# Transposing softmax exponentials in four 32-row strips of TensorE instead of two 64-row strips, under a newly written order

## The chip, the cores and the metric

The kernel runs on one core of a Trainium2 chip. The metric is the device time of one execution in microseconds (us), as the median of several runs. All durations below come from one profiled execution of the kernel before the change. Engine names are those of the profile: PE is TensorE's matmul stream and PEld its stream of weight loads, DVE is VectorE, ACT ScalarE, POOL GpSimd, SP SyncE (which issues the DMAs).

## The reference

Eight sequences of 512 tokens (width 256) go through four residual blocks, each on a layer-normed input: a cross attention over a context of 1024 tokens (16 heads of 64), a feed-forward network that picks 2 of 8 experts per sequence, a second cross attention over the same context (16 heads of 16), and a feed-forward network with weights rounded to 8 bits and activations to 16. Only the first attention is touched:

```python
scores = jnp.einsum('bhqd,bhkd->bhqk', q, k) * SCALE
attn = jax.nn.softmax(scores, axis=-1)
out = jnp.einsum('bhqk,bhkd->bhqd', attn, v)
out = out.transpose(0, 2, 1, 3).reshape(B, NQ, INNER)
return out @ w_out + b_out
```

Everything is float32.

## The kernel before

**First attention.** `first_attention` (line 591) loops over n, 8 sequences by 8 pairs of heads, and within it over i, the four tiles of 128 queries. One tile (n, i) passes through five steps:

- `scores` (L721): for both heads, scores of 128 queries (rows) by 1024 keys (columns) in two PSUM tiles (L728). Each head uses 64 rows of the array, so the two heads run side by side. VectorE takes the row minimum of the negated scores (L739), ScalarE the exponential with its row sum (L741).
- `divide` (L752), one tile later: VectorE inverts the sums (L755), GpSimd multiplies each exponential by its share, 1024 columns per head (L758).
- `turn` (L667), two tiles later: the queries stand on the partitions, but the product with the values needs keys there. TensorE transposes the tile against an identity. The exponentials are the stationary operand (the weight load), the identity the moving one. A call handles half of the keys (u = 0 or 1): 2 heads by 4 key tiles by 2 halves of the queries (w), each a transpose of 64 partitions by 128 columns into a `[128, 64]` piece (L676). The halves w lie on different rows of the array and write different PSUM banks. One PSUM tile of two banks holds the result of a call. ScalarE (u = 0, L690) or VectorE (u = 1, L688) copies it to an `et` tile in SBUF.
- `attend` (L692): for two query tiles together, values times transposed exponentials, accumulated over 8 key tiles (L699). The heads use all 128 rows and 64 columns each.
- `project` (L710) adds the output product to the residual (L486).

In between lie `queries` (pq, L602), `keys` (pk, L512 and L514) and `values` (pv, L512 and L514) for later pairs. The last two run a first chunk on 128 rows and a second one on 64.

**Second stream.** The second attention of one sequence (L937) runs beside the first attention of the next. Its steps are `scores` (L562 and L565, tile s_c) together with `maxima` (L524, tile sm_c, with a VectorE maximum, L531), both on 64 rows by 128 columns for each of two parts, `attend` (cav, L1079, 128 rows by 32 columns for each of four parts), and small transposes and projections (tm_c, cf, cta, cacc).

**What sets the order.** TensorE's program is written out by hand. Each stream is a Python generator that yields before every step, and `weave` (L53) takes steps from the two streams in turn: `ORDER` (L27) lists how many steps of the first, then of the second, then of the first. TensorE executes the steps in just this order. The lists yielded with each step hold prices for a planner that made ORDER offline: microseconds on TensorE, engine and time of the eviction, and a word for the shape of the array ("full", "rows" for 64-row parts, "columns", "slots"). In the program they have no effect: `weave` counts steps and looks only at callables. The other engines run their instructions in the order in which the steps issue them.

**Buffers.** All PSUM tiles rotate through four buffers of two banks (`ps_s`, L129). A tile waits until the tile four allocations earlier has been read. The `et` tiles share two buffers of 8 KB per partition (tag "t"), and for the last sequence the second attention's split keys (L1032) reuse them.

Of the kernel before, what the change touches and what calls it, by code (L numbers as in the profile page):

```python
# [8 lines left out]
F32 = mybir.dt.float32  # L9
I32 = mybir.dt.int32  # L10
U32 = mybir.dt.uint32
F32R = mybir.dt.float32r
# [6 lines left out]
P = 128  # L19
# [5 lines left out]


ORDER = """  # L27
15 4 11 1 1 4 3 2 2 1 5 4 3 1 8 1 6 1 3 1 3 1 3 1 1 1 1 1 6 1 3 1 1 1 1 1 1 1 3 1 1
1 1 1 3 1 1 1 5 1 1 1 3 1 1 1 1 1 3 1 1 1 1 1 1 1 3 1 1 1 1 1 1 1 4 1 91 1 4 4 6 1 3
2 6 2 4 2 7 5 4 2 1 1 4 1 1 1 1 5 1 1 5 2 3 7 1 3 6 2 3 7 1 1 1 2 6 2 3 10 1 4 1 1 5  # L30
2 3 7 1 1 1 2 5 2 1 1 1 1 3 2 2 3 5 2 1 1 3 1 1 2 4 9 2 1 3 2 11 2 4 1 7 2 2 1 3 6 3
1 1 1 5 1 1 2 4 2 5 4 6 1 4 1 2 1 3 1 1 1 5 2 3 4 6 1 3 2 6 2 4 2 7 5 4 2 1 1 4 1 1
1 1 5 1 1 5 2 3 7 1 3 6 2 3 7 1 1 1 2 6 2 3 10 1 4 1 1 5 2 3 7 1 1 1 2 5 2 1 1 1 1 3
2 2 3 5 2 1 1 3 1 1 2 4 9 2 1 3 2 11 2 4 1 7 2 2 1 3 6 3 1 1 1 5 1 1 2 4 2 5 4 6 1 4
1 2 1 3 1 1 1 5 2 3 4 6 1 3 2 6 2 4 2 7 5 4 2 1 1 4 1 1 1 1 5 1 1 5 2 3 7 1 3 6 2 3
7 1 1 1 2 6 2 3 10 1 4 1 1 5 2 3 7 1 1 1 2 5 2 1 1 1 1 3 2 2 3 5 2 1 1 3 1 1 2 4 9 2
1 3 2 11 2 4 1 7 2 2 1 3 6 3 1 1 1 5 1 1 2 4 2 5 4 6 1 4 1 2 1 3 1 1 1 5 2 3 4 6 1 3
2 6 2 4 2 7 5 4 2 1 1 4 1 1 1 1 5 1 1 5 2 3 7 1 3 6 2 3 7 1 1 1 2 6 2 3 10 1 4 1 1 5
2 3 7 1 1 1 2 5 2 1 1 1 1 3 2 2 3 5 2 1 1 3 1 1 2 4 9 2 1 3 2 11 2 4 1 7 2 2 1 3 6 3
1 1 1 5 1 1 2 4 2 5 4 6 1 4 1 2 1 3 1 1 1 5 2 3 4 6 1 3 2 6 2 4 2 7 5 4 2 1 1 4 1 1  # L40
1 1 5 1 1 5 2 3 7 1 3 6 2 3 7 1 1 1 2 6 2 3 10 1 4 1 1 5 2 3 7 1 1 1 2 5 2 1 1 1 1 3
2 2 3 5 2 1 1 3 1 1 2 4 9 2 1 3 2 11 2 4 1 7 2 2 1 3 6 3 1 1 1 5 1 1 2 4 2 5 4 6 1 4
1 2 1 3 1 1 1 5 2 3 4 6 1 3 2 6 2 4 2 7 5 4 2 1 1 4 1 1 1 1 5 1 1 5 2 3 7 1 3 6 2 3
7 1 1 1 2 6 2 3 10 1 4 1 1 5 2 3 7 1 1 1 2 5 2 1 1 1 1 3 2 2 3 5 2 1 1 3 1 1 2 4 9 2
1 3 2 11 2 4 1 7 2 2 1 3 6 3 1 1 1 5 1 1 2 4 2 5 4 6 1 4 1 2 1 3 1 1 1 5 2 3 4 6 1 3
2 6 2 4 2 7 5 4 2 1 1 4 1 1 1 6 1 1 2 4 1 1 1 3 1 2 1 3 2 1 1 2 3 3 2 5 1 1 2 6 2 3
2 1 1 6 4 5 1 1 2 6 2 3 2 1 1 7 1 4 4 5 2 4 1 7 1 5 2 3 1 2 2 3 7 1 3 4 2 3 7 2 2 1
1 1 1 1 11 2 1 1 1 1 5 1 8 1 2 3 3 1 2 1 7 3 2 4 3 8 3 1 5 2 1 7 2 3 7 2 3 7 2 3 7 3
3 9 3 2 9 3 2 6 2 1 2 1 2 1 3 1 4 2
"""  # L50


# [26 lines left out]
def kernel(  # L79
# [26 lines left out]
    nc = tc.nc  # L106
    B, S, D = x.shape
    L, DC = cross.shape[1:]
    NT = S // P
    NK = L // P  # L110
# [18 lines left out]
    ps_s = ctx.enter_context(tc.tile_pool(name="ps_s", bufs=4, space=PSUM))  # L129
# [5 lines left out]
    ident = const.tile([P, P], F32, name="ident")  # L135
# [364 lines left out]
    def tok(t):  # L500
        return slice(t * P, (t + 1) * P)
# [89 lines left out]
    def first_attention():  # L591
# [72 lines left out]
            if half and m < last // 2:  # L664
                load_weights(m + 1, "v")

        def turn(n, i, u):  # L667


            j = i // 2  # L670
            t = ps_s.tile([P, 2, 2, 4, 64], F32, tag="s", name=f"t_{n}_{i}_{u}")
            for h in range(2):
                for kt in range(4):
                    for w in range(2):
                        half = slice(w * 64, (w + 1) * 64)
                        nc.tensor.transpose(  # L676
                            t[:, w, h, kt, :],
                            es[n, i][h][half, tok(4 * u + kt)],
                            ident[half, half],
                        )  # L680
            if i % 2 == 0:
                turned[n, j, u] = pp.tile(
                    [P, 2, 4, 2, 2, 64], F32, tag="t", name=f"et_{n}_{j}_{u}", bufs=2
                )
            dst = turned[n, j, u][:, :, :, i % 2].rearrange("p h k w s -> p w (h k) s")
            src = t.rearrange("p w h k s -> p w (h k) s")
            if u:
                nc.vector.tensor_copy(dst, src)  # L688
            else:
                nc.scalar.copy(dst, src)  # L690

        def attend(n, j):  # L692

            m, at = divmod(n * 2, G)
            av = bank(f"av_{n}_{j}")
            for u in range(2):
                for kt in range(4):
                    for h in range(2):
                        nc.tensor.matmul(  # L699
                            av[h * AD : (h + 1) * AD, : S // 2],  # L700
                            v[m][:, 4 * u + kt, (at + h) * AD : (at + h + 1) * AD],
                            turned[n, j, u][:, h, kt].rearrange("p i w s -> p (i w s)"),
                            start=(u == 0 and kt == 0),
                            stop=(u == 1 and kt == 3),
                        )
            if j == 0:
                o[n] = op.tile([P, S], F32, tag="o", name=f"o_{n}", bufs=3)
            nc.scalar.copy(o[n][:, j * (S // 2) : (j + 1) * (S // 2)], av[:, : S // 2])
# [55 lines left out]
        VALUES = [(2.75, "s", "act", 1.03, "full")]  # L764
        OUT = [(3.44, "s", "dve", 1.25, "full")]
        BIAS = [(0, None, "pool", 2.9, "aside")]
        TURN = 0.55

        share = 1 / (NP * NT)

# [8 lines left out]
        def divided(g):  # L779
            return [  # L780
                (0, None, "dve", 0.2, None, (("y", g % 4),), None),
                (0, None, "pool", 4.8, "then", (), ("w", g % 4)),
            ]

        def turned_round(g, u):
            engine, took = ("dve", 1.22) if u else ("act", 1.03)
            return [(TURN, "s", engine, took, "rows", (("w", g % 4),), ("t", u, g % 4))]

        def attended(g):

# [8 lines left out]
        for n in range(last + 2):  # L799
            b, p = divmod(n, NP)  # L800
            if n == 2:
                yield lambda: "biases" in done
                yield 0, BIAS
                bias()
            for i in range(NT):
                g = n * NT + i
                if n <= last:
                    yield 0, scored(g), share
                    scores(n, i)
                if n == 0 and i < 2:  # L810
                    yield 0, VALUES
                    values(0, i)


                if g > 3 and i % 2 == 0:
                    m = (g - 4) // NT
                    yield 0, attended(g - 3)
                    attend(m, i // 2)
                if i == 1 and p == NP - 2 and b + 1 < B:
                    yield from all_of(front[1 + DH :])  # L820
                if i == 1 and n // 2 + 1 <= last // 2:
                    yield 0, VALUES
                    values(n // 2 + 1, p % 2)
                if i == 3 and n < last:
                    yield 0, KEYS
                    keys(n + 1)
                if i == 3 and n % 2 == 0 and n > 0:
                    yield 0, OUT
                    project(n // 2 - 1)
                    if p == 0 and b < B:  # L830
                        done.add(b - 1)
                if 1 < g <= last * NT + NT + 1:
                    for u in range(2):
                        yield 0, turned_round(g - 2, u)
                        turn((g - 2) // NT, (g - 2) % NT, u)
                if 0 < g <= last * NT + NT:
                    yield 0, divided(g - 1)
                    divide((g - 1) // NT, (g - 1) % NT)
                if n > last:
                    if i == 3:  # L840
                        return
                    continue
                if i == 2 and n < last:
                    yield 0, QUERIES
                    queries(n + 1)

                if b + 1 < B:
                    if p == NP - 2:
                        if i == 0:
                            yield lambda: b == 0 or (b - 1, "stacked") in done  # L850
                            front, bias = prologue(b + 1)
                        elif i == 2:
                            yield from all_of(front[:1])
                    if p == NP - 1 and i == 0:
                        yield from all_of(front[1 : 1 + DH])
                        yield 0, BIAS
                        bias()
# [79 lines left out]
    def second_attention(b, pairs, last=False):  # L937
# [78 lines left out]
        def keys_of(m):  # L1016
# [12 lines left out]
                ]  # L1029
            )  # L1030
            if b == B - 1:
                both = pp.tile([P, 2, L], F32R, tag="t", name=f"ck_{b}_{m}", bufs=2)  # L1032
                kh, kl = both[:, 0, :], both[:, 1, :]
            else:
                kh = pp.tile([P, L], F32R, tag="e", name=f"ckh_{b}_{m}")
                kl = pp.tile([P, L], F32R, tag="e", name=f"ckl_{b}_{m}")
# [435 lines left out]
```

## Time and profile before

| what | value |
|---|---|
| median of 3 runs | 3412.78 us (3411.16 to 3414.15) |
| the profiled execution | 3413.37 us, span 3411.5 us, mean granted TensorE clock 0.974 |
| TensorE (PE) busy | 3183.9 us (93%), 24293 matmuls |
| weight loads (PEld) busy | 1789.0 us, 24293 |
| VectorE, ScalarE, GpSimd busy | 2045.0, 1857.9, 1282.3 us |
| transposes of the turn (L676) | 8192 matmuls, 313.7 us busy |
| copies of the turned tiles (L688, L690) | 256 on VectorE, 1222 ns each; 256 on ScalarE, 1016 ns each |
| scores of the first attention (L728) | 2048 matmuls, 586.6 us busy |
| values times exponentials (L699) | 4096 matmuls, 472.2 us busy |
| GpSimd's multiplication (L758) | 512, 1894 ns each |

How to read it: a group's line in the profile has the source line, engine, operation, the tile written and the tiles read, the shape as rows times columns of the array, the count, the busy time, and the mean duration of one. TensorE overlaps its matmuls, so the mean of one (227 ns for a transpose) is a latency, and the busy time of the group divided by the count (38 ns) is closer to its pace. Weight loads overlap the matmuls of earlier weights. A line "a <- b" names who ended a wait. A matmul of float32 operands stands in the profile as two instructions, a transpose as one.

The first attention of the eight sequences, and beside it the second attention of the sequence before, fill the span from about 45 us to 3006 us (the first and last transposes of the turn). After that come the second attention of the last sequence and, from about 3240 us, the last feed-forward network, which the change leaves alone.

### The profile page before, as it was taken

Reading aid. Unit: us, or ns where it says so; the run is one execution under the profiler, and the core shown is the slowest. Engines: PE = TensorE matmul, PEld = TensorE weight load, DVE = VectorE, ACT = ScalarE, POOL = GpSimd, SP = SyncE. Lnnn points to the kernel's source line nnn. Section 1 sums busy time; section 2 is a strip of 40 time slices with the busy share of each in tenths; the row PEclk is TensorE's granted clock in tenths of the full one; section 3 lists DMA queues with packets and bytes.
Section 4 is the critical chain, followed back from the end, with each engine's and each line's share of the span. In section 5 each row is a group of like instructions: output and inputs, shape, how many; then the busy total and the mean of one; then the engine's idle time right before and its main releaser. Section 6 shows DMA issues by size and latency. Waiting matters only on the chain.

```text
span 3411.5 us, 59285 instructions
## 1 busy us (share of the span) xinstructions
PE 3183.9 (93%) x24293; PEld 1789.0 (52%) x24293; DVE 2045.0 (60%) x2583; ACT 1857.9 (54%) x2589; POOL 1282.3 (38%) x1260
## 2 busy tenths in 40 slices
PE   7899999999999999999999999999999999978887
PEld 4455555555455555555545554555555555544347
DVE  3654566546665476655665466654766456656688
ACT  4554456544556455554655455554555546544578
POOL 4355522454234622355224542345223543311002
PEclk9999999999999999999999999999999999988989
DMA  2010111011110111111110111101111111012112
GB/s 86 26 32 21 45 33 37 27 41 41 38 35 27 43 32 36 35 44 29 32 51 14 41 41 38 41 26 38 32 41 32 41 32 29 14 44 62 50 57 81
DMA packets 102649, 132.00 MB, mean 39 GB/s; under 512 B 19807, under 2 KB 82028, under 8 KB 102252
## 3 DMA queue, kind: packets, MB, share of 16 engines
q1 hardware_dynamic: 102380, 128.22, 13.7%
q8 instruction: 192, 3.15, 0.4%
q14 instruction: 77, 0.63, 0.1%
HBM read 67.34 MB, written 9.96 MB: 23 GB/s over the span
## 4 chain that ended last, share of the span: by engine, by line
PE 74%; DVE 12%; ACT 6%; POOL 3%; issue 2%; DMA 1%; SPq 1%; ACTq 0%; DVEq 0%; POOLq 0%
PE s L728 15%; PE av L699 11%; PE cav L1079 6%; PE t L676 6%; DVE cmx L531 5%; PE acc L486 5%; PE pv L512 4%; PE s_c L562 3%; PE pq L602 3%; PE pk L512 3%; ACT e L741 2%; ACT e_c L567 2%; PE sm_c L524 2%; PE s_c L565 2%; PE pv L514 2%
## 5 line engine op out<-in xcount | busy, mean ns | idle before, releaser
L758 POOL TENSOR_TENSOR e<-e,share 128x1024 f32<-128x1024 f32 x512 | 958.9, 1894 | 1559.1 <-DVE share L755 1528.0
L741 ACT ACTIVATE e<-s,least 128x1024 f32<-128x1024 f32 x512 | 569.6, 1113 | 621.3 <-DVE least L739 590.0
L739 DVE TENSOR_REDUCE least<-s 128x1 f32<-128x1024 f32 x512 | 603.2, 1219 | 229.5 <-PE s L728 226.4
L531 DVE TENSOR_REDUCE cmx<-sm_c 128x2 f32<-128x1024 f32 x512 | 602.1, 1219 | 169.8 <-PE sm_c L524 169.2
L728 PE MATMUL s<-k,q 64*128 64x512 f32 x2048 | 586.6, 624 | 23.0 <-ACT et L690 8.8
L567 ACT ACTIVATE e_c<-s_c 128x1024 f32<-128x1024 f32 x512 | 499.7, 1024 | 112.9 <-PE s_c L565 101.8
L699 PE MATMUL av<-et,v 128*64 128x256 f32 x4096 | 472.2, 384 | 0.7 <-ACT et L690 0.7
L688 DVE COPY et<-t 128x1024 f32<-128x1024 f32 x256 | 312.8, 1222 | 230.4 <-PE t L676 228.5
L699 PEld LDWEIGHTS av<-et,v 128*64 128x64 f32 x4096 | 284.4, 137 | 219.4 <-issue 67.9
L728 PEld LDWEIGHTS s<-k,q 64*128 64x128 f32 x2048 | 237.1, 191 | 221.1 <-issue 118.1
L676 PEld LDWEIGHTS t<-ident,e 64*128 64x128 f32 x8192 | 294.4, 141 | 93.9 <-issue 68.2
L690 ACT COPY et<-t 128x1024 f32<-128x1024 f32 x256 | 260.1, 1016 | 151.4 <-PE t L676 149.9
L676 PE MATMUL t<-ident,e 64*128 64x64 f32 x8192 | 313.7, 227 | 18.1 <-ACT e_c L567 12.1
L562 PE MATMUL s_c<-cq,ck 64*128 64x512 f32 x1024 | 248.5, 476 | 16.1 <-ACT e_c L567 10.7
L524 PE MATMUL sm_c<-ck,cq 64*128 64x512 f32 x1024 | 228.5, 442 | 25.9 <-DMA ck<-ckl 12.5
L1079 PE MATMUL cav<-e_c,cv 128*32 128x512 f32 x2048 | 248.2, 599 | 2.2 <-DVE cmx L531 1.9
L755 DVE RECIPROCAL share<-total 128x2 f32<-128x2 f32 x256 | 42.5, 166 | 298.2 <-ACT e L741 297.8
L565 PE MATMUL s_c<-m_rows,m_ones 64*128 64x512 f32 x1024 | 208.6, 396 | 2.7 <-DMA m_rows<-mr_c 2.6
L562 PEld LDWEIGHTS s_c<-cq,ck 64*128 64x128 f32 x1024 | 99.3, 187 | 165.2 <-issue 39.4
L524 PEld LDWEIGHTS sm_c<-ck,cq 64*128 64x128 f32 x1024 | 98.8, 189 | 107.5 <-DVE cmx L531 38.4
L512 PE MATMUL pv<-wv,c 128*128 128x256 f32 x512 | 131.2, 399 | 3.7 <-DMA wv<-in_L_xattn_w_kv_dram 2.4
L512 PE MATMUL pk<-c,wk 128*128 128x512 f32 x256 | 126.8, 618 | 4.5 <-DVE et L688 2.7
(202 smaller groups left out, 3382.9 us busy)
## 6 DMA issues: line engine op xcount, KB each, us to landing
cq<-cqs SPq DMA_DIRECT2D x256, 64.0 KB
ck<-ckh SPq DMA_DIRECT2D x112, 128.0 KB
ck<-ckl SPq DMA_DIRECT2D x112, 128.0 KB
wq<-in_L_xattn_w_q_dram SPq DMA_DIRECT2D x32, 256.0 KB
wo<-in_L_xattn_w_out_dram SPq DMA_DIRECT2D x32, 256.0 KB
w<-in_L_ffn_W_dram SPq DMA_DIRECT2D x32, 256.0 KB
x<-xd SPq DMA_DIRECT2D x16, 512.0 KB
ctx<-in_ctx_dram SPq DMA_DIRECT2D x16, 384.0 KB
```

The costliest lines, as they stand in the source:

```text
L512: nc.tensor.matmul(out, lhs, rhs, start=first, stop=False, skip_group_check=True)
L524: nc.tensor.matmul(s[:, h, :], q[half, tok(i)], k[half, g * 512 : (g + 1) * 512], start=True, stop=True,)
L531: nc.vector.tensor_reduce(mx[:, :, i, g], s, AX.X, ALU.max)
L562: nc.tensor.matmul(s[:, h, :], k[half, tok(kt)], q[half, :], start=True, stop=False)
L567: nc.scalar.activation(e, s, AF.Exp, scale=scale)
L676: nc.tensor.transpose(t[:, w, h, kt, :], es[n, i][h][half, tok(4 * u + kt)], ident[half, half],)
L699: nc.tensor.matmul(av[h * AD : (h + 1) * AD, : S // 2], v[m][:, 4 * u + kt, (at + h) * AD : (at + h + 1) * AD], turned[n, j, u][:, h, kt]. ...
L728: nc.tensor.matmul(s[h][:, g, :], q[n][half, tok(i)], k[n][half, g * 512 : (g + 1) * 512], start=True, stop=True,)
L739: nc.vector.tensor_reduce(least[:, h : h + 1], s[h], AX.XY, ALU.min)
L741: nc.scalar.activation(e, s[h].rearrange("p g n -> p (g n)"), AF.Exp, bias=least[:, h : h + 1], scale=-1.0, accum_out=total[:, h : h + 1],)
L758: nc.gpsimd.tensor_tensor(e, e, share[:, h : h + 1].to_broadcast([P, L]), ALU.mult)
L1079: nc.tensor.matmul(av[col : col + SL, :], va[:, v : v + SL], es[p, kt][:, h, :], start=(i == 0), stop=(i == NK // 4 - 1),)
```

## The change

A turn now handles all 1024 keys of a tile in one call. It cuts the 128 queries into four strips of 32 partitions, gives each transpose its strip of the array's rows (`tile_position`), and writes into two PSUM tiles at once, so that each strip has a bank of its own. There are 64 transposes per tile, each of 32 partitions by 128 columns against a 32 by 32 identity. The two copies follow when all of them are issued. The `et` tile covers all keys: one buffer of 16 KB in place of two of 8 KB, and the last sequence's split keys share one tile likewise. `attend` reads the same 256 contiguous columns per key tile as before.

```diff
-        def turn(n, i, u):
+        def turn(n, i):
+            t = [
+                ps_s.tile([P, 2, 2, NK, 32], F32, tag="s", name=f"t_{n}_{i}_{u}") for u in range(2)
+            ]
+            for h in range(2):
+                for kt in range(NK):
+                    for w in range(4):
+                        rows_ = slice(w * 32, (w + 1) * 32)
+                        nc.tensor.transpose(
+                            t[w // 2][:, w % 2, h, kt, :],
+                            es[n, i][h][rows_, tok(kt)],
+                            ident[rows_, rows_],
+                            tile_position=(w * 32, 0),
+                        )
             j = i // 2
...
             if i % 2 == 0:
-                turned[n, j, u] = pp.tile(
-                    [P, 2, 4, 2, 2, 64], F32, tag="t", name=f"et_{n}_{j}_{u}", bufs=2
-                )
...
+                turned[n, j] = pp.tile(
+                    [P, 2, NK, 2, 4, 32], F32, tag="t", name=f"et_{n}_{j}", bufs=1
+                )
+            for u in range(2):
+                dst = turned[n, j][:, :, :, i % 2, 2 * u : 2 * u + 2].rearrange(
+                    "p h k w s -> p w (h k) s"
+                )
+                src = t[u].rearrange("p w h k s -> p w (h k) s")
+                if u:
+                    nc.vector.tensor_copy(dst, src)
+                else:
+                    nc.scalar.copy(dst, src)
```

The planner's prices change with it: a turn is priced at two halves of 0.3 us (before: two of 0.55) in a shape of its own, "quarters", and GpSimd's division at 4.0 us (before 4.8). ORDER is written anew throughout, and the first stream yields one step per turn where it yielded two:

```diff
-        TURN = 0.55
+        TURN = 0.3
...
-                (0, None, "pool", 4.8, "then", (), ("w", g % 4)),
+                (0, None, "pool", 4.0, "then", (), ("w", g % 4)),
...
-                    for u in range(2):
-                        yield 0, turned_round(g - 2, u)
-                        turn((g - 2) // NT, (g - 2) % NT, u)
+                    yield 0, turned_round(g - 2)
+                    turn((g - 2) // NT, (g - 2) % NT)
...
-                both = pp.tile([P, 2, L], F32R, tag="t", name=f"ck_{b}_{m}", bufs=2)
+                both = pp.tile([P, 2, 2, L], F32R, tag="t", name=f"ck_{b}", bufs=1) if m == 0 else shared[b, "k"]
+                shared[b, "k"] = both
+                both = both[:, m]
```

## Prediction

> **What bounds the kernel.** I read the page's busy shares first, then the chain of work that ended last, then the rows of the turning transposes, and last the timeline around them.
>
> ```profile
> PE 3183.9 (93%) x24293; PEld 1789.0 (52%) x24293; DVE 2045.0 (60%) x2583; ACT 1857.9 (54%) x2589; POOL 1282.3 (38%) x1260
> L676 PEld LDWEIGHTS t<-ident,e 64*128 64x128 f32 x8192 | 294.4, 141 | 93.9 <-issue 68.2
> L676 PE MATMUL t<-ident,e 64*128 64x64 f32 x8192 | 313.7, 227 | 18.1 <-ACT e_c L567 12.1
> ```
>
> TensorE is busy 93% of the span, and the chain gives it 74%. So what counts is TensorE's time from step to step. The change touches one of its costly groups, the 8192 transposes of line 676, each a weight load of 64 rows by 128 columns (the exponentials) and a matmul of 64 columns (the identity). The chain shows what a step costs, since a piece ends where the next begins (start, length, step, matmuls):
>
> ```profile
> 1024.29 1.06 PE pk L514 x4
> 1025.35 3.65 PE acc L486 x16
> 1029.00 1.14 PE t L676 x32
> ...
> 1063.40 0.99 PE t L676 x32
> 1064.39 1.91 PE pq L602 x4
> ...
> 1072.11 0.99 PE t L676 x32
> 1073.10 1.85 PE cav L1079 x16
> ...
> 1082.32 1.14 PE t L676 x32
> 1083.46 1.77 PE s L728 x8
> ...
> 1099.56 1.06 PE cacc L1123 x4
> 1100.62 1.72 PE pq L602 x4
> ```
>
> The reader is to see two things. A turned tile (32 transposes) takes 0.99 us when the step before it also used 64 rows and 128 columns of the array (pk's second half, s, s_c), and 1.14 behind acc, which uses 128 rows. And pq takes 1.72 behind a step of its own shape, 1.91 behind t. So **a change of the array's shape costs about 0.15 us into t, 0.20 into pq or acc (3.65 against 16 x 0.215 = 3.44)**; in the same way 0.15 into av (3.60 against the 3.45 it takes behind cf, which has its shape), 0.13 into cav (1.85 against 1.72), and 0.20 into s. Leaving t without a change of shape costs s 0.05 (1.77). A strip of 32 rows is no exception:
>
> ```profile
> 70.31 1.06 PE pv L514 x8
> 71.37 0.15 PE tbi L326
> 71.53 1.01 PE t L676 x27
> ```
>
> tbi is one transpose of 8 rows, so it sits in one 32-row strip. It stands between two 64-row steps and costs 0.15 us, all of it change of shape.
>
> **Part 1, the transposes themselves.** 32 transposes per tile of 128 queries become 64, so 8192 become 16384, on four strips of 32 rows in place of two of 64. In both, a strip gets 16 of them. Before, they take 0.99 / 16 = 62 ns per strip. What sets the 62?
>
> ```profile
> L676 PEld LDWEIGHTS t<-ident,e x8192: 133/139/228, 45.2 to 3005.5; 64*128 64x128 f32 x200
> L326 PEld LDWEIGHTS tbi<-ident,bir x1: 134/134/134, 71.3 to 71.3; 8*128 8x128 f32 x1
> L464 PEld LDWEIGHTS td<-ident,ctx x64: 110/140/232, 17.1 to 2584.4; 128*64 128x64 f32 x32, 128*128 128x128 f32 x32
> 336.76 1.97 PE L676 MATMUL t<-ident,e 64*128 64x64 f32 x32
> 338.52 2.02 PE L728 MATMUL s<-k,q 64*128 64x512 f32 x4
> ```
>
> Two rows speak for the weight load. A transposing load of 128 columns takes 139 ns with 64 rows, 134 with 8, 140 with 128; with 64 columns it takes 110. It follows columns, not rows, and the change keeps 128 columns. And where the granted clock was 0.50 (335 to 338 us) the tile took 338.52 - 336.76 = 1.76 us, 110 ns per strip: were the 64-column matmul the limit at both clocks, full clock would give 55, not 62. So I take it that at full clock the load holds the strip. Four strips loading side by side then need 16 x 62 = 0.99 us again. **The tile gains nothing**, though the matmul behind each load halves. The ends: if the matmul were the limit after all, 32 columns would take 62 - 27 = 35 ns (27 being half of 110 / 2, the streaming it saves), 0.57 us a tile, -0.42 x 256 = -108 us. If TensorE can start no more than one transpose per 31 ns, the densest long stretch the trace holds (0.99 / 32), 64 take 1.98, +253 us. I choose 0, by the load rows, the nearest to the disputed operation.
>
> Against the upper end stands a short burst: eight loads of about 110 ns each in 0.16 us, some 7 ns apart.
>
> ```profile
> 437.70 0.16 PEld L1079 LDWEIGHTS cav<-e_c,cv 128*32 128x32 f32 x8 [0.24 <-issue]
> ```
>
> The new tile needs 64 loads and 64 matmuls in 0.99 us, 7.7 ns an instruction, eight times as long as that burst of loads; the trace does not show it sustained. The Trainium skill speaks on both sides here. "TensorEngine Tiling (Array Packing)", section "Theoretical Speedup", promises up to 4x for a dimension of 32 or less, which would make the tile about half of the two-strip one. "TensorE: Matmul & The Clock Gate", section "Wait — 56ns, not 53.3ns?", says that starts never come closer than about 25 ns however small the matmul; taken as a limit over all strips that is an estimate of 64 x 25 = 1.6 us a tile, about 155 us more in all. The load rows speak against the first and the burst against the second.
>
> **Part 2, changes of shape.** The turn now always stands alone: nothing else of the main stage but the one-row bias steps uses 32 rows and 128 columns. I laid out the steps of both streams from the loops and counted neighbours under both ORDER lists. Before: 262 runs of turning steps, 98 entered and 95 left by a change of shape, 167 left without. After: 256 runs, 254 entered and 256 left by one. In all 1224 changes become 1523. At the prices above: into t 98 x 0.15 = 14.7 becomes 254 x 0.15 = 38.1, **+23.4 us**. Out of t, 95 changes (16.2 us) and 167 unchanged exits at 0.055 to 0.07 (9.9) are 26.1; 256 changes (173 into s and the scores at 0.197, 51 into pq and other full steps at 0.20, the rest cheaper) are 48.0, **+21.9**. All other neighbours 179.1 against 175.7, **-3.4**. Sum +42 us.
>
> **Part 3, the rest of the new order.** Runs of score-and-maximum steps without another step between are held by VectorE (1.22 us a maximum, 0.7 of TensorE). Their excess by length, from the timeline, is 0.15, 0.84, 0.92 and 2.24 us for runs of 1, 2, 3 and 5 (1.6 for 4, between its neighbours). Before there are 56, 73, 61 and 11 (no 4), 150 us; after 68, 39, 52, 12 and 18, 150 us. Nothing changes.
>
> **Part 4, PSUM, copies, buffers.** Both halves of a tile are now open at once, two of four buffers, and the ScalarE copy starts with the VectorE copy, half a turn (0.5 us) later. The copies move the same 1024 elements (1016 and 1222 ns), so 0. Where scores follow, a later copy can hold the third score tile by up to 0.5 us, at 50 such exits up to +25; I take half, +12. On the other side, s right behind pv and t takes 2.25 to 2.68 us from its start to that of the av behind it, where 1.92 is free of waiting (26 times), because it waits for pv's buffer; a turn that begins and ends later eats into that wait: up to 0.3 us at some 65 places behind pv, acc, cpk and route, -20 at most; I take -15. One et buffer of 16 KB in place of two of 8 costs nothing: TensorE does the attend that reads it before the transposes that refill it, in order. The prices TURN and 4.0 only fed the plan. No DMA is added; instructions grow by 16384 on queue q8, whose 3.15 MB take 0.4%.
>
> **Sum.** 0 + 42 + 0 + 12 - 15 = +39 us on the profiled execution's 3413.4 (span 3411.5, 1.9 around it): 3452. The median shown, 3412.8, is 0.6 below it; I predict **3452 us**. Its own range is 3425 to 3480 (waits at either end, counting errors).
>
> **Rivals.** *A, the matmul was the limit* (faster): the tile falls to 0.57 us, -108 + 39 gives 3344. For it: the streams halve. Against: the load rows. It decides once a strip's period falls under 62 - 39000 / (256 x 16) = 52 ns. Chance 0.12. *B, issue is the limit*: between 15.4 ns and 31 ns per transpose. At 20 the tile takes 1.28, +74 + 39 gives 3526; at 31 it gives 3705. For it: nothing denser is sustained in the trace; against: the burst. Chance 0.20, of which 0.07 above 3620. *C, the changes of shape are eaten by waits that are there anyway* (TensorE's gaps come to 228 us, 18 in every 395 us of the main stage): 3400 to 3420, chance 0.09, of which 0.04 faster and 0.05 the same. The forecast has 0.59.
>
> So: faster by over 0.2% (under 3406) 0.12 + 0.04 = 0.16; within 0.2%, about what a measurement here tells from no change, 0.05; slower 0.59 + 0.20 = 0.79. The range leaves out A and the top of B (0.12 + 0.07): 3395 to 3620.
>
> **What would show it.** The loads of t: still about 135 ns with 32 rows; a whole t piece of 64 near 1.14 us in the chain (0.99 and the entry). pq and s behind t at 1.91 to 1.97. A piece near 0.7 is A; one of 1.4 or more is B, its load starts evenly spaced at over 15 ns. If the piece is 1.14 and the time still stands near 3413, look for shorter s steps behind t (C). I would be most wrong if a 32-row load frees its strip sooner than its duration tells.

## The result, and the profile after

The changed kernel takes 3462.5 us (median, 3458.6 to 3472.8) against 3413.5 of the kernel before in the same comparison: a ratio of 1.0149, 95% interval 1.0136 to 1.0161, **49 us slower**. The forecast was 3452. The profiled execution took 3458.6 us, span 3456.7.

The page of the changed kernel, busy shares and the rows of the turn (rows times columns of the array, count, busy us, mean ns):

```profile
PE 3216.7 (93%) x32485; PEld 1799.6 (52%) x32485; DVE 2048.0 (59%) x2583; ACT 1852.5 (54%) x2575; POOL 1282.9 (37%) x1260
L676 PEld LDWEIGHTS t<-ident,e 32*128 32x128 f32 x16384 | 283.3, 137 | 120.6 <-issue 104.7
L676 PE MATMUL t<-ident,e 32*128 32x32 f32 x16384 | 313.5, 223 | 11.9 <-ACT v L659 3.6
```

Twice as many transposes keep the matmul stream busy for the same time, 313.5 us against 313.7, and a load takes 137 ns against 141 though it has half the rows. The turn gained nothing. In the starts of the trace a strip takes a new transpose every 62 ns, the number of before, now on four strips at once: 64 transposes from first start to last in 0.975 us.

The chain of the changed kernel shows what stands around a turn:

```profile
1041.32 1.37 PE t L676 x58
1042.69 1.91 PE pq L601 x4
...
1053.89 1.14 PE t L676 x63
1055.03 2.16 PE s L733 x8
...
1062.54 1.17 PE t L676 x58
1063.71 0.04 issue
1063.75 1.03 ACT et L695
1064.78 0.04 issue
1064.82 0.50 PE s_c L561 x2
...
1080.51 1.12 PE t L676 x53
1081.63 1.91 PE s L733 x7
```

Behind pv's 64-row half (1080.51) a turn now takes 1.12 us where it took 0.99, and s behind it 1.91 where 1.77 was possible. These are the forecast changes of shape. The piece at 1063.75 is something else: the chain runs through ScalarE's copy of the turned tile, because the next score tile waits for the PSUM buffer that this copy empties. TensorE does not stand still for the whole of the 1.03 us. It still runs scores into other buffers, and the timeline has it idle for 0.26 us:

```profile
1064.82 0.50 PE L561 MATMUL s_c<-cq,ck 64*128 64x512 f32 x2 [0.26 <-ACT et L695]
```

From 520 to 1360 us such copies stand on the chain 11 times (11.1 us); before, twice (1.8 us).

### The profile page after: what moved, and what is told of

Same layout as the page of the kernel before. It is cut to its first block, busy times and chain, and to the rows that moved or that the text cites. A ratio compares the mean times of both kernels' runs of the same rounds, so it can differ in the third digit from the quotient of the medians.

```text
span 3456.7 us, 75724 instructions
## 1 busy us (share of the span) xinstructions
PE 3216.7 (93%) x32485; PEld 1799.6 (52%) x32485; DVE 2048.0 (59%) x2583; ACT 1852.5 (54%) x2575; POOL 1282.9 (37%) x1260
## 4 chain that ended last, share of the span: by engine, by line
PE 77%; DVE 11%; ACT 7%; issue 2%; POOL 1%; DMA 1%; SPq 1%; ACTq 0%; DVEq 0%; POOLq 0%
PE s L733 14%; PE av L704 13%; PE t L676 7%; PE cav L1087 6%; PE acc L485 5%; DVE cmx L530 4%; PE s_c L561 4%; PE pq L601 4%; PE pv L511 3%; PE pk L511 3%; PE s_c L564 2%; ACT e L746 2%; PE sm_c L523 2%; ACT e_c L566 2%; PE ph L925 2%; PE pv L513 2%
## 5 line engine op out<-in xcount | busy, mean ns | idle before, releaser
L733 PE MATMUL s<-k,q 64*128 64x512 f32 x2048 | 578.7, 621 | 9.1 <-ACT k L632 4.4
L693 DVE COPY et<-t 128x1024 f32<-128x1024 f32 x256 | 312.9, 1222 | 286.8 <-PE t L676 286.6
L704 PEld LDWEIGHTS av<-et,v 128*64 128x64 f32 x4096 | 292.5, 138 | 236.4 <-issue 82.7
L695 ACT COPY et<-t 128x1024 f32<-128x1024 f32 x256 | 259.7, 1014 | 261.0 <-PE t L676 257.1
L676 PEld LDWEIGHTS t<-ident,e 32*128 32x128 f32 x16384 | 283.3, 137 | 120.6 <-issue 104.7
L676 PE MATMUL t<-ident,e 32*128 32x32 f32 x16384 | 313.5, 223 | 11.9 <-ACT v L659 3.6
```

The source lines that it names most:

```text
L676: nc.tensor.transpose(t[w // 2][:, w % 2, h, kt, :], es[n, i][h][rows_, tok(kt)], ident[rows_, rows_], tile_position=(w * 32, 0),)
L704: nc.tensor.matmul(av[h * AD : (h + 1) * AD, : S // 2], v[m][:, 4 * u + kt, (at + h) * AD : (at + h + 1) * AD], turned[n, j][:, h, 4 * u + ...
L733: nc.tensor.matmul(s[h][:, g, :], q[n][half, tok(i)], k[n][half, g * 512 : (g + 1) * 512], start=True, stop=True,)
```

## The experiments

Times are compared with the kernel before in the same comparison (3411.2, 3410.6 or 3411.3), so each run is quoted by its difference.

**1. The strips alone, on the old order.** All 64 transposes stand where the second half-turn stood:

```diff
                     for u in range(2):
                         yield 0, turned_round(g - 2, u)
-                        turn((g - 2) // NT, (g - 2) % NT, u)
+                        if u:
+                            turn((g - 2) // NT, (g - 2) % NT)
```

with `turn`, the et buffer and the split keys as in the changed kernel.

> The old order, with all 64 transposes on four strips issued at the place of the second half-turn. Theory (the strips cost because each turn now stands between two changes of the array's shape): counted on the old order, the changes cost 219.9 us before and 267.5 with strips, so +48 us, about 3461; the turn itself keeps 62 ns per strip and load. Rival 1 (the new order costs, the strips are neutral): about 3413. Rival 2 (two PSUM tiles open at once and the late ScalarE copy cost): above 3461, by as much as the run with late copies and two strips is above 3413.

Measured: 3452.1, **+40.8** (ratio 1.0121, 1.0104 to 1.0138). This is below the 3461 that the changes of shape alone were to give. The new order is not the main cause. But the next two runs show that the strips aren't all of it either.

**2. The new order alone**, with two strips of 64 rows, both PSUM tiles open from the start and complete only at the end:

```diff
-                ps_s.tile([P, 2, 2, NK, 32], F32, tag="s", name=f"t_{n}_{i}_{u}") for u in range(2)
+                ps_s.tile([P, 2, NK, 64], F32, tag="s", name=f"t_{n}_{i}_{h}") for h in range(2)
...
+            for kt in range(NK):
+                for h in range(2):
+                    for w in range(2):
+                        half = slice(w * 64, (w + 1) * 64)
+                        nc.tensor.transpose(t[h][:, w, kt, :], es[n, i][h][half, tok(kt)], ident[half, half])
```

> The new order, with the old two strips of 64 rows (32 transposes per tile, both halves in one call, both copies at the end). Theory: 219.7 us of changes of shape, as before (219.9), so about 3413, and at most 15 more by the late copies. Rival 1 (the new order costs): about 3460.

Measured: 3429.5, **+18.3** (1.0051, 1.0034 to 1.0068), between the two.

**3. The same call on the old order.**

> The old order and the old two strips, but both halves of a turn in one call, two PSUM tiles open at once, and both copies only after the last transpose. Theory: 3413 to 3425. Rival 2 (open tiles and late copies are what costs): 3440 to 3460.

Measured: 3437.5, **+26.2** (1.0075, 1.0058 to 1.0092). My theory put this at 12 at most. With two strips, no shape changed, so opening both tiles at once and finishing both late costs something of its own, and the strips add only 40.8 - 26.2 = 14.6 on this order.

**4. Fewer changes of shape, nothing else.** ORDER rewritten by exchanges of neighbours; the kernel before otherwise.

> The kernel before with 178 exchanges of neighbouring steps in its order, none moved by more than one place against the other stream, chosen to put steps of one shape together: 1225 changes of shape become 1124, 219.9 us of them 199.8. Theory (a change costs its 0.10 to 0.20 us wherever it stands): about 3393. Rival (changes are mostly eaten by waits that are there anyway, or the exchanges break the plan's covers): 3413 or more.

Measured: 3626.2, **+215** (1.064, 1.0617 to 1.0663). It fell through entirely. Waits of TensorE, first in the kernel before, then in this run (us in total, times, longest):

```profile
PE sm_c L524 <- ACT e L741: 1.5, 6, 0.3
```

```profile
PE s_c L560 <- ACT e L739: 65.7, 53, 1.9
PE sm_c L522 <- ACT e L739: 32.7, 51, 1.8
PE av L697 <- ACT e L739: 20.5, 20, 1.9
```

Steps of the second attention, and the first attention's product with the values (av), now wait for the first attention's exponentials, the instructions that read the score tiles out of PSUM. The three rows are 119 us of the 215; the largest row of this run is another one, txn waiting for POOL's xn, 85.5 us where it was 49.1. What the rest is made of was not followed up. For the question at hand: an order with 100 changes of shape fewer can be far slower, so their count alone forecasts nothing when the order moves.

**5 to 7. What it is in the call of run 3.** Same old order, same two strips, same buffers; only the sequence of the transposes within the call differs (the three added lines are those of run 5, run 6 and run 7, in this order, each in place of the two removed ones):

```diff
-            for kt in range(NK):
-                for h in range(2):
+            for h, kt in [(h, kt) for h in range(2) for kt in range(NK)]:
+            for h, kt in [(0, 0), (1, 0)] + [(h, kt) for h in range(2) for kt in range(1, NK)]:
+            for h, kt in [(0, kt) for kt in range(NK - 1)] + [(1, kt) for kt in range(NK)] + [(0, NK - 1)]:
```

> The old order and two strips, one call per tile, one 16 KB et buffer, the halves cut by head; the first PSUM tile is finished half way through the call and the second is not touched before that, as in the kernel before. Theory (in the run with the old order and late copies, 26 us came from the two PSUM tiles, not from the merged call or the et buffer): 3411 to 3415. Rival (the merged call or the one et buffer costs): about 3437.

> As the run with early copies, but the first four transposes go two to each PSUM tile, so that TensorE needs both buffers when the turn starts; the first tile is still finished nearly half way through. If needing the second buffer half a turn earlier is what costs: 3430 to 3437. If the later ScalarE copy is: 3411 to 3415.

> As the run with early copies, but the last two transposes of the first PSUM tile are issued at the very end, so that its copy starts about half a us later; the second buffer is still needed only near the middle. If the later ScalarE copy is what costs: 3430 to 3437. If the early need of the second buffer is: 3411 to 3415.

Measured: run 5 3406.4, **-4.3** (0.9989, 0.9979 to 0.9998); run 6 3419.1, **+8.5** (1.0026, 1.0015 to 1.0037); run 7 3424.1, **+13.4** (1.0041, 1.0027 to 1.0055). The merged call and the one et buffer cost nothing. Needing the second PSUM buffer at once costs 12.8, the late copy 17.7, and together 30.5: just what run 3 lies above run 5 (26.2 + 4.3). Either of my expectations alone was wrong; it is both.

The timeline's starts say where. In run 6 a turn behind scores of the second attention takes 1.27 us in the mean against 1.14 in run 5 (79 turns in both), and 1.00 behind pv in both. The time is lost in front of the third transpose, the first one into the second tile: TensorE waits for that buffer. Who held it the profile names only in some of these turns (ScalarE's copy of v in 7, VectorE's maximum of the scores in 4). In run 7 these turns are as in run 5 (1.14), but from the last transpose's start to the end of the scores behind it 3.05 us pass against 2.85 (47 times, second attention) and 2.65 against 2.56 (114 times, first attention). On the chain from 520 to 1360 us ScalarE's copy of a turned tile stands twice in run 5, twice in run 6 and 23 times in run 7. The waits of s_c for that copy, in its weight load (PEld) and its matmul (PE), run 5 and then run 7:

```profile
PEld s_c L562 <- ACT et L691: 26.0, 58, 0.8
PE s_c L562 <- ACT et L691: 1.9, 6, 0.3
```

```profile
PEld s_c L562 <- ACT et L691: 44.7, 58, 1.1
PE s_c L562 <- ACT et L691: 16.9, 46, 0.7
```

The same 58 places wait longer, and the matmul itself now waits 46 times in place of 6.

**8. The new order with early copies**, the sequence of run 5 in the changed kernel:

> The new order with two strips, and the first PSUM tile finished half way, the second needed only from there. The late copies cost 26 us on the old order; the new order with them takes 3430. If the new order is by itself as good as the old one: 3405 to 3415; if it was planned for tiles that open together and gains little from early copies: 3420 to 3430. Under 3405 it would beat both kernels.

Measured: 3397.2, **-13.4** (0.9962, 0.9948 to 0.9976). This is below both of my ranges and beats both kernels. The new order is better than the old by 9 us here (-13.4 against -4.3) and by 8 with late copies (18.3 against 26.2), and worse by 8 with the strips it was planned for (49.0 against 40.8). The last pair comes from two comparisons, whose intervals are some 4 and 6 us to either side; the other two pairs were each run side by side.

**9 and 10. What sets the 62 ns.** The loads cut to half their columns; rows, moving columns, counts and order are kept (run 9 shown):

```diff
+        et_all = pp.tile([P, 2, NK, 2, 4, 32], F32, tag="t", name="et_all", bufs=1)
+        nc.gpsimd.memset(et_all, 0.0)
...
-                            t[w // 2][:, w % 2, h, kt, :],
-                            es[n, i][h][rows_, tok(kt)],
+                            t[w // 2][0:64, w % 2, h, kt, :],
+                            es[n, i][h][rows_, kt * P : kt * P + 64],
```

> The changed kernel with the weight load of each transpose cut from 128 to 64 columns: it leaves out the upper half of every key tile, so the output is not the attention's. The count of loads and matmuls, the 32 rows, the 32 moving columns, the copies' lengths and the order stay. Theory (the load's columns set the 62 ns per strip): the period falls to 28 to 36 ns, a turn to about 0.55 us, at most 0.45 x 256 = 115 us less than the changed kernel's 3460, less what waits take back. Rival (a fixed time per pair of load and matmul on a strip, or the rate at which 64 pairs can be issued): the period stays at 62 and the time at 3460.

> The same cut of the loads from 128 to 64 columns in the new order with two strips and late copies (3430); the upper half of every key tile is left out here too. Theory: the load no longer holds the strip, the 64-column matmul does, at half of the 110 ns that it took at half clock: 55 ns, a turn of 0.88 us in place of 0.99, 28 us less, about 3402. Rival (a fixed time per pair): 62 ns and 3430.

Measured: run 9 3396.3 (**-15.0**; 0.9946, 0.9923 to 0.9969), 64 us under the changed kernel; run 10 3410.6 (-0.8; 0.9996, 0.9985 to 1.0008), 19 under run 2. The turn's instructions and one turn in the timeline (start, length), first of the changed kernel, then of run 9:

```profile
L676 PEld LDWEIGHTS t<-ident,e x16384: 132/137/224, 45.1 to 3051.7; 32*128 32x128 f32 x200
...
1080.44 1.19 PE L676 MATMUL t<-ident,e 32*128 32x32 f32 x64
1081.56 1.98 PE L733 MATMUL s<-k,q 64*128 64x512 f32 x7
```

```profile
L679 PEld LDWEIGHTS t<-ident,e x16384: 102/108/154, 44.7 to 2988.9; 32*64 32x64 f32 x200
...
1040.45 0.72 PE L679 MATMUL t<-ident,e 32*64 32x32 f32 x64
```

With the same 32 moving columns, half the columns of the load bring the turn from 1.19 to 0.72 us, latency of the last matmul included, and in the starts of the trace the period of a strip from 62 to 33 ns. On two strips with 64 moving columns it goes to 56 only: there the matmul takes over, at the 55 forecast from the half-clock stretch. So the load's columns are the limit at full clock.

The turns that fell into stretches at half clock say the same of the load. In run 1, where 32 columns move in place of 64, a turn at a granted clock of 0.50 (739 to 743 us) stands in the timeline as

```profile
740.94 1.92 PE L677 MATMUL t<-ident,e 32*128 32x32 f32 x64
742.79 2.08 PE L734 MATMUL s<-k,q 64*128 64x512 f32 x4
```

and in the starts of all seven such turns of run 1 a strip takes a transpose every 107 ns, just as in the seven of the kernel before. Run 9, with half of both, has 53 in its one such turn, and run 10, with half the load and 64 moving columns, 107. So at half clock a load of 128 columns and a matmul of 64 columns take the same 107 ns each.

"TensorE: Matmul & The Clock Gate" of the Trainium skill, section "LDWEIGHTS (loading the stationary operand)", says the same of the load, that it is priced by its columns and not by the rows it covers; run 9 is the measurement for 32 rows.

Of the 0.47 us that run 9 saves in each of 256 turns (120 us), 64 arrive, and of the 28 us forecast for run 10, 19.

## Why the prediction was right, and where it was not

The sum was 39 us and 49 came. By terms, on the new order and with the differences of the runs:

| term | forecast | measured | from |
|---|---|---|---|
| the transposes themselves | 0 | 0 | 62 ns per strip before and after |
| strips: changes of shape, less what does not arrive | +42 - 15 = +27 | +30.7 | changed kernel minus run 2 |
| second buffer at once, late copies | +12 | +31.7 | run 2 minus run 8 |
| new order, merged call, one et buffer | 0 | -13.4 | run 8 |
| sum | +39 | +49.0 | |

The changed kernel and run 2 come from two comparisons, and so do run 2 and run 8; the +30.7 and the +31.7 are known to some 7 us.

**Part 1 was right, by the row it chose.** The load holds the strip; the copies' lengths did not move (1222 and 1014 ns). Two of the supports were weaker than they looked. The 110 ns at half clock was put down to the matmul alone, but run 1 has the same 107 with half the moving columns, so that stretch could not tell the load from the matmul. And the 140 ns read for a load of 128 rows is the median of two forms of td taken together; the row for that size alone is tc's, and it says the same:

```profile
L457 PEld LDWEIGHTS tc<-ident,ctx x64: 138/141/231, 16.2 to 2583.6; 128*128 128x128 f32 x64
```

Rival A falls: the period stayed at 62, not 35, and runs 9 and 10 show why. Rival B falls: 64 loads and 64 matmuls run in 0.975 us, and in run 9 in 0.53, 8 ns per transpose. What I called unshown, that the rate of the burst can be sustained, holds over the whole turn. The estimate from the floor of about 25 ns between starts ("TensorE: Matmul & The Clock Gate" of the Trainium skill, section "Wait — 56ns, not 53.3ns?") does not hold across strips: starts here are 15 ns apart in the mean, and the measurement decides. Nor did the strips bring anything of the up to 4x of "TensorEngine Tiling (Array Packing)", section "Theoretical Speedup": twice the strips had twice the loads, each still of 128 columns and 62 ns.

**Part 2 was right in its counts and nearly right in its prices.** From the end of the last matmul before a change to the end of the first one behind it the changed kernel takes 174 ns into t and 623 into s. Less the streaming of that first matmul (27 ns for 32 columns; 429 for 512, the spacing of s's matmuls on one strip) this is 147 and 194, at the counted places (123 turns before s, 65 behind av, 44 behind pv). But the streaming counts too. The first transpose now streams 32 columns where it streamed 64, so an entry that was free of a change rose from 49 to 174 ns (behind pv and pk), by 125 and not by 150, and one that had a change already fell from 203 to 174 (behind av and acc). Over 256 turns that is some 7 us that the forecast did not take off.

That waits would eat part of the changes was right as well, and the part depends on the order. About 42 - 31 = 11 us do not arrive on the new one, some 4 beyond those 7; on the old order 48 - 15 = 33, some 26 beyond them. On the old order it can be seen where, from run 3 to run 1: with strips a turn behind pv goes from 1.00 to 1.13 us and behind acc from 1.04 to 1.17, but behind second-attention scores it stays at 1.27, where in 29 and 28 of the 79 turns TensorE waits for the second buffer anyway; and s behind a turn ends its first matmul only 85 ns later in the mean (114 turns), where a change without waiting costs 623 - 482 = 141. That the missing 26 us are waits altogether is argued from these places and not shown for each.

**Part 3 failed in "Nothing changes".** I compared the runs of scores alone and found them equal. The new order is 8 to 9 us better with either kind of copy, and the merged call gives another 4 on the old one. Why the new order is better was not followed up.

**The step of Part 4 that failed is "at 50 such exits up to +25; I take half, +12".** The late copy costs 17.7 us on the old order, which the bound would have covered. But the other half of the same change, TensorE needing both buffers when the turn starts, I named and did not price, and it costs 12.8. On the new order the two together cost 31.7 and were not run apart. Part 4 was too low by 19.7 there, and the order's gain, which I set at 0, took 13.4 off again; so it is partly luck that the total came out close, and it says less for the forecast than the number suggests. "TensorEngine Tiling (Array Packing)", section "Gotcha 1: PSUM Pressure", states that row tiles write different banks and raise the pressure on PSUM. Four strips, each with a bank of its own, indeed made the turn hold two of the four buffers at once. The 31.7 us, measured with two strips in the same two buffers, are the price of needing both at the start and finishing both at the end. What happens when two strips share a bank, or when four strips finish one tile early, was not tried.

Rival C, that the changes vanish in waits, is refuted for the change as a whole; for the strips on the old order it would have been about half true, if the missing 26 of 48 us are waits.

## What to carry to other kernels

Before splitting a transpose over more row strips, ask which operand the strip waits for: if it is the weight load, and its columns stay, more strips do the same work in the same time and add a change of the array's shape on both sides. Price what the split does to PSUM as well: how many buffers a step must hold when it starts, and when the first of them is complete, counted by who stands behind it. In this kernel, with two strips, the sequence of the same transposes inside one call was worth 30 us, as much as the strips cost on the new order, and finishing one tile early was free.

## What the runs showed of the hardware

- A transposing float32 load of 128 columns takes nearly the same time with 8, 32, 64 and 128 rows (134, 137, 139, 141 ns), and four of them on different strips run side by side without slowing: 62 ns per strip with two strips and with four.
- With half the columns a strip took such a load every 33 ns in place of 62 at full clock, and every 53 in place of 107 where the granted clock was 0.50 (runs 9 and 1).
- TensorE sustained one load and one matmul every 15 ns for a whole turn, and every 8 ns in run 9.
- Entering the 32-row shape costs what entering the 64-row shape costs: 147 ns against 149 before a transpose, the streaming of the first one taken off.
